# Root rows added by accumulating gathers in the last edge group of a relational graph layer, with a longer count for the group's pace

## The chip, the cores and the metric

One core of one Trainium2 chip. The metric is the device time of one execution in microseconds (us), the median of the runs; before the change it is 1372.6 us over 3 runs (1371.87 to 1372.61).

## The reference, cut to what matters

There are 1250 nodes with 1024 features each, 20000 edges and 8 edge types, all in float32. h is the rectified layer norm of x. For every type r, the rows h[src] of the edges of that type are averaged at each destination node and multiplied by a 1024 x 1024 matrix. The rest is a gate:

```
u   = h @ root + bias + sum over r of mean_r(h[src]) @ weight[r]
z   = concat(u, h) @ w_gate + b_gate
out = x + tanh(u) * z + h * (1 - z)
```

## The kernel before, in words

**Blocks and stages.** The nodes lie in ND = 10 blocks of 128 (the last has 98). TensorE does eleven products of all nodes with one 1024 x 1024 matrix: the eight edge types (stages s = 0 to 7), the root matrix (s = 8), the lower half of the gate matrix (s = 9, its result is called z) and the upper half applied to u (s = 10, the gate stage). Stages 0 to 9 run through `step`, one step for each of NP = 5 pairs of blocks; the gate stage is the loop at the end. Each step is a Strassen-like product in seven parts (`product`, L341): A11, S1, S2, then p3, p7 and p2 (in an order that depends on the step), then A22. After each part `done()` calls the hook `between(j)` with j = 0 to 6, and the hook writes other work into the engines' instruction streams. The instruction order is the program's own; every engine runs its stream in order.

**What the products leave.** Stage results go to DRAM: y for the edge types, `hr_dram` for the root product, `z_dram` for z. Edge types 0 to 4 are one group and 5 to 7 the other; edges of a group are gathered after its products are there.

**Slots.** A node's edges of one group lie in slots, and nodes are sorted by degree, so block d needs K[g][d] slots: for the last group (g = 1) K = 20, 10, 8, 7, 7, 6, 5, 5, 4, 3, in all 75. `add_slot` (L1162) writes one indirect gather on GpSimd (POOL) of 128 rows of y into a tile `got` (L1165), and one multiply-add on VectorE (DVE) that puts it into the block's sum u (L1170). There are GOT = 4 `got` tiles, shared by all gathers of this part, and UB = 4 tiles u.

**The order of the last group.** `edges` (L1188) is a generator; one advance is one tick t, from -1 to 85. It runs through the blocks in the order 4 to 9, then 0 to 3. With starts[b] the first tick of a block, a block's u is read at starts[b] - 5 by `first_u` (a gather from `u_dram`, what the first group left), its slots follow one in each tick, and 4 ticks after the last slot the block leaves through `to`. For blocks 4 to 9 that is `to_last`, a write to `last_dram`. For blocks 0 to 3, which are held on the chip (HELD = 4), it is `add_hr` (L1375): a gather of the block's rows of `hr_dram` into a `got` tile, and three ticks later an addition on DVE (L1380). The starts are ticks 34, 54, 64 and 72 for blocks 0, 1, 2 and 3; block 3's last slot is tick 78, its `hr_dram` gather tick 82, its addition tick 85.

**The pace.** `spread` (L1220) spreads `total` ticks over `parts` calls of the hook: after the k-th of 70 parts (stages 8 and 9, 5 steps of 7 parts each) ceil(total k / 70) ticks have been written, and at the last part all that are left. total is 75 + 2 + 4 = 81; tick -1 is written ahead of it.

**The gate stage.** In the last step of stage 9 `gate_u(0, j)` already reads the rows of h that belong to pair 0 (blocks 0 and 1) into `got` tiles (j = 2), takes tanh of u (L1445) and transposes u on TensorE (L322; j = 3), and subtracts the rows of h from tanh (L1453; j = 4). `gate_bias(0)` (L1418, two writes of b_gate into the place of z) is called there at j = 0. In the gate stage, step i writes: at j = 0 two gathers of `xh_dram` and, by `gate_load(i + 2, 0)`, two loads of u from `last_dram` on SP and two `hr_dram` gathers; at j = 2 the additions L1380 of those, and the rows of h and tanh for pair i + 1; at j = 3 the transposes of pair i + 1. z is added onto the bias by accumulating gathers (L586 with an add, from `z_dram`) at j = 3 of the first step, and j = 0 of the later ones. L373 is the addition that drains part p3 out of its PSUM bank, L381 and L389 those of p7 and p2. Step order in this stage and in the last step of stage 9: A11, S1, S2, p3, p7, p2, A22.

Of the kernel before, what the change touches and what calls it, by code (L numbers as in the profile page):

```python
# [13 lines left out]
OP = mybir.AluOpType  # L14
# [5 lines left out]
def tile_rgcn_highway(  # L20
# [44 lines left out]
    NP = ND // 2  # L65
# [4 lines left out]
    K = ((28, 14, 13, 12, 11, 10, 9, 8, 7, 6), (20, 10, 8, 7, 7, 6, 5, 5, 4, 3))  # L70
# [9 lines left out]
    GOT = 4  # L80
    UB = 4
    LATE = 4
# [7 lines left out]
    def nrows(d):  # L90
        return min(P, N - d * P)
# [4 lines left out]
    def nedges(c):  # L96
        return P if c < NCH - 1 else EL
# [10 lines left out]
    hr_dram = dram.tile([N, D], F32, name="hr_dram")  # L108
# [332 lines left out]
    NM = len(mats)  # L441
# [130 lines left out]
    node = const.tile([P, G, ND], I32, name="node")  # L572
# [11 lines left out]
    def rows_of(to, of, at, op=OP.bypass):  # L584

        nc.gpsimd.indirect_dma_start(  # L586
            out=to, out_offset=None, in_=of,
            in_offset=bass.IndirectOffsetOnAxis(ap=at, axis=0), compute_op=op)
# [53 lines left out]
    with ExitStack() as early:  # L642
# [20 lines left out]
        class Normed:  # L663
# [13 lines left out]
            def spread(self):  # L677
                n = self.n
                nc.vector.bn_aggr(self.mv[:n], self.st[:n].rearrange("p a b -> p (a b)"))
                nc.scalar.activation(self.sd[:n], self.mv[:n, 1:2], AF.Sqrt, bias=eps[:n])  # L680
# [70 lines left out]
        for name, of, pad in (("dst", dst, G * KEYS), ("typ", etype, R), ("src", src, 0)):  # L751
            t = ix0.tile([P, 2, P], I32, name=f"e_{name}")
# [374 lines left out]
        while going[0]:  # L1127
            s, i = next(steps)
# [11 lines left out]
    with ExitStack() as edges_part:  # L1140
# [21 lines left out]
        def add_slot(u, g, d, k, at, w):  # L1162
            n = nrows(d)
            t = got()
            nc.gpsimd.indirect_dma_start(  # L1165
                out=t[:n], out_offset=None, in_=y[g][:, :],
                in_offset=bass.IndirectOffsetOnAxis(ap=at[:n, d, k:k + 1], axis=0),
                bounds_check=y[g].shape[0] - 1, oob_is_err=False)
            w = w[:n, d, k:k + 1]
            nc.vector.scalar_tensor_tensor(u[:n], t[:n], w, u[:n], op0=OP.mult, op1=OP.add)  # L1170

        us = {}

        def new_u(d):

            return upool.tile([P, D], F32, name="u")

        def first_u(g, d):

            n = nrows(d)  # L1180
            u = new_u(d)
            if g == 0:
                nc.sync.dma_start(u[:n], bias[None, :].to_broadcast([n, D]))
            else:
                rows_of(u[:n], u_dram[g - 1][:, :], node[:n, g, d:d + 1])
            return u

        def edges(g, blocks, to, late=0):  # L1188

            nb = len(blocks)
            starts = [late + sum(K[g][d] for d in blocks[:b]) for b in range(nb + 1)]
            leaves = [starts[b + 1] - 1 + GOT for b in range(nb)]
            reads = [max(-1, starts[b] - 5, leaves[b - UB] if b >= UB else -1) for b in range(nb)]
            u, then = {}, {}
            for t in range(-1, leaves[-1] + 4):
                for b, d in enumerate(blocks):
                    if starts[b] <= t < starts[b + 1]:  # L1200
                        k = t - starts[b]
                        add_slot(u[d], g, d, k, idx[:, g], w_of[:, g])
                for b, d in enumerate(blocks):
                    if t == leaves[b]:
                        then[t + 3] = to(d, u[d])
                if then.get(t):
                    then[t]()
                for b, d in enumerate(blocks):
                    if t == reads[b]:
                        u[d] = first_u(g, d)  # L1210
                yield

        def u_back(g):
# [47 lines left out]
        def beside(e, total, s, i, last):  # L1261


            between = spread(e, total, 7 * ((last - s) * NP + NP - i))
            while s <= last:
                step(s, i, between)
                s, i = next(steps, (NM, 0))
            return s, i

        s, i = next(steps)  # L1270
        while s <= EARLY:
            step(s, i)
            s, i = next(steps)
# [17 lines left out]
        while s < R0[1]:  # L1291
            step(s, i, on)
            s, i = next(steps)

        def with_ready(e):

            for _ in e:
                next(ready, None)
                yield

        first_group = with_ready(edges(0, range(ND), u_back(0), LATE))
        next(first_group)
        s, i = beside(first_group, sum(K[0]) + LATE + 1, s, i, R0[2] - 1)
# [4 lines left out]
        with tc.If(passes > 0):  # L1308
# [34 lines left out]
            with tc.For_i(0, passes, 1):  # L1343
# [9 lines left out]
                for c in range(NCH):  # L1353
                    n = nedges(c)
# [13 lines left out]
        LG = G - 1  # L1368
        HELD = 4
# [45 lines left out]
        def gate_bias(i):  # L1415

            for part, d, n in pair(i):
                nc.sync.dma_start(place_of("z", i, part)[:n],  # L1418
                                  b_gate[None, :].to_broadcast([n, D]))
# [19 lines left out]
        def gate_u(i, j):  # L1439

            if j == 2:
                for part, d, n in pair(i):
                    hs[part] = got()
                    rows_of(hs[part][:n], h_dram[:, :], node[:n, LG, d:d + 1])
                    nc.scalar.activation(place_of("d", i, part)[:n], us[d][:n], AF.Tanh)  # L1445
            elif j == 3:
                for part, d, n in pair(i):
                    transposed(h_op[i % 2], part, us.pop(d), n)
                left(h_op[i % 2])
            elif j == 4:  # L1450
                for part, d, n in pair(i):
                    dt = place_of("d", i, part)
                    nc.vector.tensor_sub(dt[:n], dt[:n], hs[part][:n])  # L1453

        def gate_load(i, j):
# [6 lines left out]
            elif j == 2:  # L1462
                while adds:
                    adds.pop(0)()

        blocks = [*range(HELD, ND), *range(HELD)]
        last = edges(LG, blocks, lambda d, u: (add_hr if d < HELD else to_last)(d, u), LATE)
        next(last)
        between = spread(last, sum(K[LG]) + 2 + LATE, 7 * ((NM - 2 - s) * NP + NP - i))
        while s < NM - 1:  # L1470
            def beside_h(j):
                between(j)
                if (s, i, j) == (NM - 2, NP - 1, 0):
                    gate_bias(0)
                if (s, i) == (NM - 2, NP - 1):
                    gate_u(0, j)

            step(s, i, beside_h)
            s, i = next(steps, (NM, 0))

        for i in range(NP):
            t = [rows.tile([P, D], F32, name="row") for _ in range(2)]

            def finish(part, of, c0, more=None):
                d = 2 * i + part
                n = nrows(d)
                at = slice(c0, c0 + of.shape[-1])
                to = t[part][:n, at]
                if more is None:
                    nc.vector.tensor_mul(to, of[:n], place_of("d", i, part)[:n, at])  # L1490
                    nc.vector.tensor_add(to, to, place_of("z", i, part)[:n, at])
                else:
                    nc.vector.tensor_mul(more[:n], of[:n], place_of("d", i, part)[:n, at])
                    nc.vector.tensor_add(to, to, more[:n])
# [38 lines left out]
            if i < NP - 1:  # L1533
                product(h_op[i % 2], fac[NM - 1], t, between=beside_u,
                        last=lambda *of: finish(1, *of))
# [28 lines left out]
```

## Time and profile before

| | |
|---|---|
| median of 3 runs | 1372.6 us |
| the profiled execution's own time | 1373.07 us |
| its span, first to last instruction | 1371.1 us |
| TensorE (PE) matmul busy | 1344.4 us, 98% of the span |
| DVE busy | 944.2 us, 69% |
| POOL busy | 587.3 us, 43% |
| ScalarE (ACT) busy | 370.4 us, 27% |
| mean granted TensorE clock | 0.993 |
| stage 8, 975 to 1096 us | PE busy 121.00 of 121 us, DMA share 0.80 |
| stage 9, 1096 to 1218 us | PE busy 118.94 of 122 us, DMA share 0.66 |
| gate stage and tail, 1218 to 1371 us | PE busy 132.74 of 153 us, clock 0.94, DMA share 0.67 |

In the profile, a line of the timeline gives the start in us, the length in us, the engine, the line of the kernel, the instruction with its tiles, how many were merged, and in square brackets how long the engine had been idle before it and which instruction released it. A waits line gives in total us, how often, and the longest. A windows line gives, for a stretch, its length and then each engine's busy time (with the instruction count in brackets), the granted clock, the busy share of the DMA engines and their rate in GB/s.

### The profile page before, as it was taken

What the parts mean: (1) busy time and instruction counts of PE and PEld (TensorE: products, weight loads), DVE (VectorE), ACT (ScalarE), POOL (GpSimd) and SP (SyncE); (2) the same over time, 40 slices, a digit from 0 to 9 for tenths busy, and PEclk for the clock granted to TensorE, in tenths of its full rate; (3) what the DMA queues carried; (4) which work ended last, traced back from release to release, by engine and by line L of the source; (5) the groups of instructions that cost most, each with busy time, mean ns of one, the idle gap of its engine ahead of it and who ended that gap; (6) DMA issues with size and microseconds to landing.
All of it is one profiled execution on the core that took longest, in us unless ns stands there. A gap on an engine that the chain in (4) does not pass through costs nothing.

```text
span 1371.1 us, 13215 instructions
## 1 busy us (share of the span) xinstructions
PE 1344.4 (98%) x3954; PEld 686.5 (50%) x3954; DVE 944.2 (69%) x1932; ACT 370.4 (27%) x816; POOL 587.3 (43%) x510
## 2 busy tenths in 40 slices
PE   9999999999999999999999999999999999986997
PEld 5444455455445545554554554555455455543443
DVE  6855967876795743426767776877776796656875
ACT  3335566565731111111111111111112111120210
POOL 0001655654562475002444554455356364435641
PEclk9999999999999999999999999999999999998999
DMA  8755766854954351135549689878678936859971
GB/s 306 275 180 149 92 140 142 213 78 116 194 138 109 71 146 22 61 138 184 191 129 329 218 265 354 271 272 294 209 241 317 360 101 219 308 200 280 328 212 58
DMA packets 106908, 271.15 MB, mean 198 GB/s; under 512 B 22692, under 2 KB 24946, under 8 KB 106704
## 3 DMA queue, kind: packets, MB, share of 16 engines
q1 hardware_dynamic: 46640, 120.01, 29.8%
q0 software_dynamic: 44064, 118.28, 27.4%
q10 hardware_dynamic: 16128, 31.98, 7.4%
q8 instruction: 31, 0.51, 0.2%
q14 instruction: 45, 0.37, 0.1%
HBM read 212.71 MB, written 75.66 MB: 210 GB/s over the span
## 4 chain that ended last, share of the span: by engine, by line
PE 75%; issue 9%; DMA 9%; POOL 4%; DVE 2%; SPq 0%; POOLq 0%; ACT 0%; DVEq 0%; ACTq 0%
PE ps L356 60%; PE ps L214 8%; DMA got<-y,idx 6%; PE ps_n L356 3%; DMA got<-hr_dram,node 2%; PE ps_q L214 2%; POOL got L1165 1%; PE ps_n L214 1%; POOL got L586 1%; DMA w<-in_L_gnn_weight_dram 1%; POOL out_dram L592 1%; PE ps_n L903 1%; PE ps L322 0%; POOL h_op L586 0%; POOL w L586 0%
## 5 line engine op out<-in xcount | busy, mean ns | idle before, releaser
L356 PE MATMUL ps<-w,h_op 128*128 128x512 f32 x2512 | 1110.3, 595 | 13.6 <-DVE row L373 11.3
L356 PEld LDWEIGHTS ps<-w,h_op 128*128 128x128 f32 x2512 | 472.7, 191 | 558.2 <-issue 528.4
L1165 POOL DMA_INDIRECT got<-y,idx x193 | 250.6, 1298 | 357.8 <-DVE u L1170 230.8
L1170 DVE SCALAR_TENSOR_TENSOR u<-got,w_of,u 128x1024 f32<-128x1024 f32 (+1 forms) x193 | 247.0, 1282 | 85.5 <-DMA got<-y,idx 82.6
L982 POOL DMA_INDIRECT table<-row_col,at_i x157 | 176.6, 1125 | 157.7 <-DVE at_i L978 73.9
L381 DVE TENSOR_TENSOR row<-row,part 128x512 f32<-128x512 f32 x55 | 37.9, 689 | 123.8 <-ACT part L380 123.8
L429 ACT COPY row<-ps 128x512 f32<-128x512 f32 x50 | 29.3, 585 | 215.5 <-PE ps L356 215.5
L380 ACT COPY part<-ps 128x512 f32<-128x512 f32 x55 | 32.2, 586 | 179.7 <-PE ps L356 179.7
L395 ACT COPY row<-ps 128x512 f32<-128x512 f32 x55 | 32.2, 585 | 175.4 <-PE ps L356 170.7
L214 PE MATMUL ps<-w,w 128*128 128x256 f32 x288 | 71.3, 380 | 0.0
L406 ACT COPY row<-ps 128x512 f32<-128x512 f32 x55 | 32.2, 586 | 139.3 <-PE ps L356 139.3
L214 PEld LDWEIGHTS ps<-w,w 128*128 128x128 f32 x288 | 54.4, 190 | 18.3 <-issue 12.4
L968 DVE SCALAR_TENSOR_TENSOR junk<-k_bc,key_col,before 128x128 f32<-128x128 int32 x157 | 54.9, 350 | 4.2
L908 DVE TENSOR_TENSOR seen<-seen,ps_n 128x100 f32<-128x100 f32 x157 | 40.3, 256 | 24.6 <-PE ps_n L903 20.4
L402 ACT COPY row<-ps 128x512 f32<-128x512 f32 x43 | 25.2, 586 | 115.7 <-PE ps L356 112.1
L214 PE MATMUL ps<-w,h_op 128*128 128x256 f32 x216 | 56.0, 382 | 0.0
L214 PEld LDWEIGHTS ps<-w,h_op 128*128 128x128 f32 x216 | 40.5, 190 | 25.6 <-issue 22.3
L169 DVE TENSOR_TENSOR w<-w,w 128x2048 f32<-128x2048 f32 (+1 forms) x12 | 25.4, 2116 | 39.3 <-PE ps L356 38.2
L885 ACT ACTIVATE is_lo<-io,less_lo 128x128 bf16<-128x128 f32 x157 | 50.2, 391 | 0.7 <-DMA xh_dram<-xt 0.7
L373 DVE TENSOR_TENSOR row<-row,ps 128x512 f32<-128x512 f32 x30 | 20.5, 684 | 37.5 <-PE ps L356 31.3
L623 POOL DMA_INDIRECT node_dram<-ids,pos_i x20 | 28.5, 1426 | 41.1 <-issue 41.1
L356 PE MATMUL ps_n<-w,h_op 128*128 128x512 f32 x96 | 43.2, 592 | 0.0
(215 smaller groups left out, 1183.1 us busy)
## 6 DMA issues: line engine op xcount, KB each, us to landing
y<-row SPq DMA_DIRECT2D x72, 512.0 KB
w<-in_L_gnn_weight_dram ACTq DMA_DIRECT2D x21, 1024.0 KB
w<-in_L_gnn_weight_dram SPq DMA_DIRECT2D x10, 1024.0 KB
k_bc<-keys_dram SPq DMA_DIRECT2D x39, 256.0 KB
l_bc<-los_dram SPq DMA_DIRECT2D x39, 256.0 KB
w<-in_L_gnn_w_gate_dram ACTq DMA_DIRECT2D x6, 1024.0 KB
h_dram<-h_op SPq DMA_DIRECT2D x9, 512.0 KB
u<-in_L_gnn_bias_dram SPq DMA_DIRECT2D x9, 512.0 KB
```

Source lines behind the costliest of these rows:

```text
L214: nc.tensor.matmul(p, a[:, k, :], b[:, k, :], start=(fresh and k == 0), stop=(k == 1), skip_group_check=True)
L356: nc.tensor.matmul(b[:, at], aop[:, i, k, :], w.of[i][:, k, at], start=(fresh and k == 0), stop=(k == KQ - 1), skip_group_check=True)
L380: nc.scalar.copy(d, b)
L381: nc.vector.tensor_add(c22, c22, d)
L395: nc.scalar.copy(c11, b)
L406: nc.scalar.copy(c12, b)
L885: nc.scalar.activation(is_lo[:, i, :], io, AF.Abs, bias=less_lo[:, c0 + i:c0 + i + 1])
L908: nc.vector.tensor_add(seen[j][:, i, :], was, p[:, i, :])
L968: nc.vector.scalar_tensor_tensor(junk, o["k_bc"][:, i, :], key_col[:, c:c + 1], before, op0=OP.is_equal, op1=OP.mult, accum_out=rank[:, c: ...
L982: ins = nc.gpsimd.indirect_dma_start(out=table[:, :], out_offset=bass.IndirectOffsetOnAxis(ap=at_i[:n, i:i + 1], axis=0), in_=row_col[:n, ...
L1165: nc.gpsimd.indirect_dma_start(out=t[:n], out_offset=None, in_=y[g][:, :], in_offset=bass.IndirectOffsetOnAxis(ap=at[:n, d, k:k + 1], axis=0),
L1170: nc.vector.scalar_tensor_tensor(u[:n], t[:n], w, u[:n], op0=OP.mult, op1=OP.add)
```

## The change

`edges` takes a dictionary `more`: a block in it has its u read nine ticks ahead of its first slot instead of five, and four ticks ahead of it `more[d]` is called on u. For blocks 1, 2 and 3 that call is `first_hr`, an accumulating gather of the block's rows of `hr_dram` straight onto u. When these blocks leave, `keep_u` only notes the tile; their `got` tile, the separate gather and the DVE addition are gone. Block 0 keeps `add_hr`. The count of the pace becomes LATE + 75 + GOT + 4 = 87, and `gate_bias(0)` is called at j = 4 instead of j = 0 of the last step of stage 9.

```diff
-        def edges(g, blocks, to, late=0):
+        def edges(g, blocks, to, late=0, more={}):
...
-            reads = [max(-1, starts[b] - 5, leaves[b - UB] if b >= UB else -1) for b in range(nb)]
+            reads = [max(-1, starts[b] - (9 if d in more else 5),
+                         leaves[b - UB] if b >= UB else -1) for b, d in enumerate(blocks)]
...
                     if t == reads[b]:
                         u[d] = first_u(g, d)
+                    if d in more and t == starts[b] - 4:
+                        more[d](d, u[d])
...
+        def with_hr(d):
+            return 0 < d < HELD
+
+        def first_hr(d, u):
+            n = nrows(d)
+            rows_of(u[:n], hr_dram[:, :], node[:n, LG, d:d + 1], OP.add)
+
+        def keep_u(d, u):
+            us[d] = u
+
         blocks = [*range(HELD, ND), *range(HELD)]
-        last = edges(LG, blocks, lambda d, u: (add_hr if d < HELD else to_last)(d, u), LATE)
+        last = edges(LG, blocks, lambda d, u: (keep_u if with_hr(d) else add_hr if d < HELD
+                                               else to_last)(d, u), LATE,
+                     {d: first_hr for d in blocks if with_hr(d)})
         next(last)
-        between = spread(last, sum(K[LG]) + 2 + LATE, 7 * ((NM - 2 - s) * NP + NP - i))
+        between = spread(last, LATE + sum(K[LG]) + GOT + 4, 7 * ((NM - 2 - s) * NP + NP - i))
...
-                if (s, i, j) == (NM - 2, NP - 1, 0):
+                if (s, i, j) == (NM - 2, NP - 1, 4):
                     gate_bias(0)
```

## The prediction

> **What bounds the kernel now.** I began with the busy shares: TensorE is busy for 98% of the span, so whatever is to be won lies in the places where it waits. The waits of PE over the last 372 us are four, and all lie where stage 9 goes over into the gate stage:
>
> ```profile
> PE ps L356 <- DVE row L373: 11.3, 2, 8.8
> PE ps L322 <- DVE u L1380: 2.7, 1, 2.7
> PE ps L356 <- DVE h_op L327: 0.9, 1, 0.9
> ```
>
> Then the timeline of PE there; the brackets hold the idle time and its releaser.
>
> ```profile
> 1204.21 3.60 PE L356 MATMUL ps<-w,h_op 128*128 128x512 f32 x8
> 1210.32 7.13 PE L356 MATMUL ps<-w,h_op 128*128 128x512 f32 x16 [2.50 <-DVE row L373]
> 1218.35 14.00 PE L356 MATMUL ps<-w,h_op 128*128 128x512 f32 x32 [0.90 <-DVE h_op L327]
> 1232.18 1.04 PE L322 MATMUL ps<-ident,u 128*128 128x128 f32 x8
> 1235.94 1.32 PE L322 MATMUL ps<-ident,u 128*128 128x128 f32 x8 [2.72 <-DVE u L1380]
> 1237.06 5.10 PE L356 MATMUL ps<-w,h_op 128*128 128x512 f32 x8
> 1250.97 23.92 PE L356 MATMUL ps<-w,h_op 128*128 128x512 f32 x48 [8.81 <-DVE row L373]
> 1274.72 1.91 PE L322 MATMUL ps<-ident,u 128*128 128x128 f32 x16
> ```
>
> Neither L373 nor L327 is slow; DVE reaches them late, because it runs in order and stands behind something else. The timeline of DVE names it:
>
> ```profile
> 1208.38 1.28 DVE L1170 SCALAR_TENSOR_TENSOR u<-got,w_of,u 128x1024 f32<-128x1024 f32 x1 [4.20 <-DMA got<-y,idx]
> 1216.41 1.28 DVE L1170 SCALAR_TENSOR_TENSOR u<-got,w_of,u 128x1024 f32<-128x1024 f32 x1 [6.14 <-DMA got<-y,idx]
> 1234.66 1.23 DVE L1380 TENSOR_TENSOR u<-u,got 128x1024 f32<-128x1024 f32 x1 [2.71 <-DMA got<-hr_dram,node]
> 1246.60 1.23 DVE L1380 TENSOR_TENSOR u<-u,got 128x1024 f32<-128x1024 f32 x1 [8.51 <-DMA got<-hr_dram,node]
> ```
>
> The first two are the slots of ticks 76 and 77, the third block 3's root rows, the fourth block 4's. On POOL one sees why they come so late: gathers wait for a free `got` tile.
>
> ```profile
> 1217.96 0.99 POOL L1165 DMA_INDIRECT got<-y,idx  x1 [7.03 <-DVE u L1170]
> 1227.50 2.47 POOL L586 DMA_INDIRECT got<-hr_dram,node  x1 [8.54 <-DVE u L1380]
> ```
>
> Of four tiles, block 2's root rows hold one from 1193.90 to 1226.88 and the rows of h two, so the last slots go one at a time. Then everything falls into one stretch. The windows:
>
> ```profile
> 1200.00:1208.00 8.00, 7.81 (x31) 4.06 (x29) 2.62 (x2) 4.39 (x6) 3.10 (x2) 1.00 1.01 391
> 1222.00:1226.00 4.00, 4.00 (x11) 1.78 (x10) 4.00 (x4) 1.02 (x2) 0.00 (x0) 1.00 0.00 0
> 1242.00:1246.00 4.00, 0.16 (x1) 0.00 (x0) 0.00 (x0) 0.59 (x1) 0.00 (x0) 1.00 1.02 401
> 1250.00:1254.00 4.00, 3.03 (x4) 1.49 (x5) 3.83 (x7) 0.00 (x0) 2.80 (x3) 0.50 0.74 233
> ```
>
> At 1222 the DMA engines move nothing; at 1242 they are full. The last line shows a second cost: after the wait of 8.8 us the granted clock is 0.50.
>
> **What these stalls cost.** From one start to the next, against the undisturbed pitch: 56 matmuls from 1302.25 to 1326.29 are 24.04 us, 0.4293 each. p7, p2 and A22 (24 matmuls) take 1218.35 - 1204.21 = 14.14 for 10.30: 3.84 lost. The transposes, 1232.18 to 1237.06, take 4.88, where the next ones take 1302.25 - 1300.50 = 1.75: 3.13. p7 and the wait, to 1250.97, 13.91 for 3.43: 10.48. The next 48 matmuls 23.75 for 20.61: 3.14, the clock alone. Sum 20.59 us.
>
> **The pace.** Before, 81 ticks go over 70 parts, 1.157 each; the last slot (tick 78, the 79th advance) comes at part 68, inside the last step of stage 9, and ticks 81 to 85 in one burst at part 70. With 87, 1.243 each, ceil(87 x 63 / 70) = 79: the last slot is written at part 63, before that step begins, and no burst is left. So L373 and L327 of that step have no slot ahead of them. DVE's lag is to be added: tick 72 was written at part 63 (A22 ends near 1188.7) and done at 1192.7, and slots issued then took 8 to 13 us to land (1189.26 to 1197.85; 1195.29 to 1208.33). I put the last slot at 1193 to 1200; L373 can run from 1202.5 and is needed at 1207.8. The 3.84 go.
>
> In stages 8 and 9 a tick now comes every 2.80 us (122 us / 35 / 1.243) instead of 3.01. By the end of stage 8, 44 advances stand there and not 41: three slots, 3 x 1.28 us of DVE and 1.5 MB. DMA was at 0.96 to 0.99 and 351 to 355 GB/s between 1051 and 1099, so a slot more there (0.5 MB) is 1.5 us of delay. PE hides it: DVE waited for slots up to 4.4 us in stages 8 and 9 before 1204, and PE waited for nothing. Without that cover it costs what it is, 0 to 4.5 us; I take 0, as these rows do.
>
> **The root rows.** Removed: three plain gathers into `got` and three L1380, 3 x 1.22 = 3.7 us of DVE, hidden but for block 3's, the 3.13 above. Added: three accumulating gathers. The nearest rows are those of z:
>
> ```profile
> L586 POOL DMA_INDIRECT h_op<-z_dram,node x6: 1549/1636/2080, 1251.8 to 1324.1; - x6
> ```
>
> 1.64 us of POOL against 1.07 for a plain one: 3 x 0.57 = 1.7 us more, beside 58 of 122 us of POOL in stage 9. Where such gathers run, the full engines move 166 to 248 GB/s, against 391 to 419 with plain ones, so each costs some 1.2 us more of DMA: 3.7 us in a stage whose DMA share is 0.66. An accumulating gather must have the rows of u landed, and POOL's later slots stand behind it. Five slots lie between, 14 us at pace, against landings of 5 to 13 us; with four slots in flight DVE feels nothing. Its own landing has four ticks, 11 us, to block 1, 2 or 3's first slot; z's, issued at 1260.87 and 1262.74, were read at 1269.12 with a wait of 0.3, so 6 to 8 us. Cost: 0, or 3 x 2 = 6 us where a landing of 13 us overruns 11 by 2 and DVE's cover is gone; I take 0, as z's rows are the nearest. `hr_dram` is complete at 1096.7 plus a landing; block 1's rows are asked for at tick 50, part 41, near 1117. The `got` tile that was held is what the last slots lacked.
>
> The Trainium skill speaks against this step: "DMA: Bandwidth & Descriptors", section "Rules for kernel authors", says that an accumulating DMA reads its destination and writes it later, and has to wait for the earlier DMA's semaphore. No run yet shows that wait; taken as one full landing of 13 us for each block and uncovered, it would add 39 us.
>
> **The gate stage's first step.** Blocks 4 and 5 keep L1380, so I follow what they wait for. Their gathers need the two `got` tiles of h, free after L1453. DVE is then at part p7: L381 near 1208.5, L173 2.3 us, L1453 to 1213.7; the gathers leave by 1215. SP's loads of u stand behind the two z writes, and these behind L389 (1214.4) and A22's copy (1215.5); they leave near 1216.5. From 1213 on the queues hold hr, z, u and the next bias, 1 MB each: 4 MB at 390 GB/s end near 1224. L1380 is over by 1227; L373 is first possible at 1228.8 and needed before p2 at 1234. Margin 7 us, against 12.3 us of landing before, when 6.5 MB met. So the 10.48 go, and the 3.14 with them. Late next: step 1's own L1380, now 3 us earlier against p2, since L1453 runs 1.4 us after p2's start instead of 4.5.
>
> The clock term, weighed once more: the skill's "TensorE: Matmul & The Clock Gate", section "Part 1: The HAM clock gate", has the clock halved after an idle window of some 3.4 us. The 0.50 after 8.8 us agrees; 0.74 to 0.83 behind the 2.7 us wait does not. By the rule p7's 1.7 us (5.10 for 3.43) would stay, and the sum be 18.9.
>
> **Gate bias.** On SP nothing stands between j = 0 and j = 4 of that step, and its data are free: it should still leave behind the z writes at 1191. If it did come later, 1 MB less at the peak of 391 GB/s is 2.6 us of landing for others. I take 0.
>
> **Sum.** 1373.07 - 20.6 = 1352.5 us for the profiled execution; it stood 0.5 above the median, so 1352.0.
>
> **Rivals.** (1) Part of the wait before p2 stays, behind block 4's rows. For it: 8.51 us of DVE there, full queues. Against: the margin of 7 us. A rest of 4 us with a clock loss of 3.1 gives 1359; all of it (13.6) 1365.6. Chance 0.20. (2) The quicker pace makes new waits in stages 8 and 9, up to 4.5 us: 1353 to 1357. Chance 0.08. (3) Slower: the accumulating gathers land so late that DVE stands before the first slot of blocks 1, 2 and 3, and PE behind it. PE pays what exceeds 4.4 us; three such waits eat the gain from 4.4 + 20.6 / 3 = 11.3 us each, that is a landing of 22 us; at 25 us three times 14 - 4.4 = 29 us, so 1381. No gather here took over 13 us. Chance 0.06. (4) The pace doesn't bite, because slots go at the rate of four tiles per landing: four in 13 us are 3.25 us a tick, slower than 2.80; the last slots stay where they were, and nothing moves: 1372. Chance 0.04, as most landings are 5 to 9 us. The forecast keeps 0.62.
>
> A measurement of this kernel can tell about 0.2%, 2.7 us, from no change. Faster: 0.62 + 0.20 + 0.08 = 0.90; same 0.04; slower 0.06. The floor is PE without waits, 1352.0, less 1.5 for what the pitch may miss; the range goes up into rival 1, to 1363: 1350.5 to 1363.
>
> **What will show it.** Right: no L1170 on DVE after 1202; seven L1380 instead of ten; PE with no wait over 1 us between 1190 and 1300, the clock 1.00 there; three L586 `u<-hr_dram` near 1117 to 1165, DVE not waiting behind them. Wrong: L373 still releasing PE, a wait for `u<-hr_dram`, or PE waits before 1190.

## The result, and the profile after

The changed kernel takes 1353.43 us (median of 4 executions, 1352.52 to 1362.24), the kernel before beside it 1372.61 us (1371.87 to 1372.80). Three of the four lie at 1352.5 to 1353.9 us and one at 1362.24 us; the record lists two more executions, at 1356.31 and 1363.04 us. The ratio is 0.9886, with a 95% interval of 0.9846 to 0.9926; it is the mean of all six over the mean of the kernel before (1356.83 / 1372.47), while the medians of the four give 0.9860. The profile is of the execution of 1362.24 us (span 1360.2 us), so it shows both what went and what came. These are its waits of PE after 900 us; the columns are total us, times, longest.

```profile
PE ps L356 <- ACT row L402: 4.1, 1, 4.1
PE ps_n L356 <- DVE row L309: 1.6, 1, 1.6
PE ps L356 <- issue: 0.7, 1, 0.7
PE ps_q L214 <- DVE inner L275: 0.5, 1, 0.5
```

No wait for L373, L327 or a root-row addition is left. Three waits are new: L402, L309 and L275; the 0.7 us of issue stand in the kernel before as well. The timeline of PE over the same stretch as before:

```profile
1187.85 13.90 PE L356 MATMUL ps<-w,h_op 128*128 128x512 f32 x32
1205.82 6.54 PE L356 MATMUL ps<-w,h_op 128*128 128x512 f32 x8 [4.08 <-ACT row L402]
1212.19 1.91 PE L322 MATMUL ps<-ident,u 128*128 128x128 f32 x16
1213.94 24.20 PE L356 MATMUL ps<-w,h_op 128*128 128x512 f32 x56
1237.98 1.91 PE L322 MATMUL ps<-ident,u 128*128 128x128 f32 x16
1239.72 24.20 PE L356 MATMUL ps<-w,h_op 128*128 128x512 f32 x56
```

From 1213.94 on, 56 matmuls take 24.04 us, start to start: the whole goes over into the gate stage without a gap, where before 20.6 us were lost. The loss now sits ahead of it: from 1187.85 to 1212.19 40 matmuls take 24.34 us instead of 17.17, so 7.17 us, of which 4.08 are the wait and the rest the clock behind it (eight matmuls in 6.54 instead of 3.60; the granted clock is 0.50 from 1206 to 1209). With 1.57 us for L309 and 0.52 for L275 these are 9.3 of the 9.7 us by which this span exceeds the forecast floor of 1371.1 - 20.6 = 1350.5.

The timeline of DVE shows that the last slot is over at 1201 and that L373 has nothing ahead of it; it is late only because PE is.

```profile
1199.98 1.28 DVE L1170 SCALAR_TENSOR_TENSOR u<-got,w_of,u 128x1024 f32<-128x1024 f32 x1 [0.20 <-DMA got<-y,idx]
1212.45 0.69 DVE L373 TENSOR_TENSOR row<-row,ps 128x512 f32<-128x512 f32 x1 [8.99 <-issue]
1232.15 1.23 DVE L1383 TENSOR_TENSOR u<-u,got 128x1024 f32<-128x1024 f32 x1 [3.74 <-DMA u<-last_dram]
1238.25 0.69 DVE L373 TENSOR_TENSOR row<-row,ps 128x512 f32<-128x512 f32 x1 [1.99 <-PE ps L356]
```

L1383 is L1380 of before. What L402 waited for is told by the chain that ended last (start, us, what):

```profile
1194.94 0.41 DVE row L245
1195.35 0.61 DVE row L309
...
1195.97 9.11 DMA z_dram<-row
...
1205.18 0.59 ACT row L402
...
1205.82 6.54 PE ps L356 x8
```

L402 is ScalarE's copy of part S1 out of PSUM into a row tile. There are four row tiles (`rows`, bufs = 4), two a step. The tile that L402 needs in the last step of stage 9 holds a result of step 2, which is finished only at the end of step 3, by L309, and then written to `z_dram`. Until that write has landed, 9.1 us after SP issued it, L402 can't start; p3 goes on in the bank that L402 reads, so PE stands too. In the kernel before the same write left at 1189.05 and L402 ran at 1195.80, right behind PE:

```profile
1189.05 2.19 SPq L475 DMA_DIRECT2D z_dram<-row  x3
1195.80 0.59 ACT L402 COPY row<-ps 128x512 f32<-128x512 f32 x1 [2.80 <-PE ps L356]
```

L309 is late after the change because DVE has five slots to add just ahead of it, four of them back to back:

```profile
1187.01 5.12 DVE L1170 SCALAR_TENSOR_TENSOR u<-got,w_of,u 128x1024 f32<-128x1024 f32 x4
1193.73 1.28 DVE L1170 SCALAR_TENSOR_TENSOR u<-got,w_of,u 128x1024 f32<-128x1024 f32 x1 [0.68 <-DMA got<-y,idx]
1195.27 0.68 DVE L309 TENSOR_TENSOR row<-row,ps_n 128x512 f32<-128x512 f32 x1
```

DVE comes to these slots late, since ahead of them it had waited longer for others to land. These are its waits for slots between 970 and 1204 us, before and after:

```profile
DVE u L1170 <- DMA got<-y,idx: 36.9, 24, 4.4
DVE u L1170 <- DMA got<-y,idx: 51.2, 23, 7.5
```

### The profile page after: what moved, and what is told of

Same layout as the page of the kernel before. It is cut to its first block, busy times and chain, and to the rows that moved or that the text cites. A ratio compares the mean times of both kernels' runs of the same rounds, so it can differ in the third digit from the quotient of the medians.

```text
span 1360.2 us, 13211 instructions
## 1 busy us (share of the span) xinstructions
PE 1343.3 (99%) x3954; PEld 686.7 (50%) x3954; DVE 940.9 (69%) x1929; ACT 370.2 (27%) x816; POOL 583.6 (43%) x510
## 4 chain that ended last, share of the span: by engine, by line
PE 76%; DMA 10%; issue 8%; POOL 4%; DVE 2%; SPq 0%; ACT 0%; POOLq 0%; DVEq 0%; ACTq 0%
PE ps L356 61%; PE ps L214 8%; DMA got<-y,idx 6%; PE ps_n L356 2%; PE ps_q L214 2%; DMA got<-hr_dram,node 2%; POOL got L1165 1%; PE ps_n L214 1%; DMA w<-in_L_gnn_weight_dram 1%; DVE u L1170 1%; DMA z_dram<-row 1%; POOL got L586 1%; POOL h_op L586 1%; PE ps L322 1%; POOL out_dram L592 1%
## 5 line engine op out<-in xcount | busy, mean ns | idle before, releaser
L1165 POOL DMA_INDIRECT got<-y,idx x193 | 247.3, 1281 | 345.3 <-DVE u L1170 212.1
L1170 DVE SCALAR_TENSOR_TENSOR u<-got,w_of,u 128x1024 f32<-128x1024 f32 (+1 forms) x193 | 246.9, 1282 | 88.8 <-DMA got<-y,idx 86.3
L395 ACT COPY row<-ps 128x512 f32<-128x512 f32 x55 | 32.2, 585 | 163.1 <-PE ps L356 157.9
L406 ACT COPY row<-ps 128x512 f32<-128x512 f32 x55 | 32.2, 586 | 133.3 <-PE ps L356 133.3
L402 ACT COPY row<-ps 128x512 f32<-128x512 f32 x43 | 25.1, 585 | 124.7 <-PE ps L356 108.1
L908 DVE TENSOR_TENSOR seen<-seen,ps_n 128x100 f32<-128x100 f32 x157 | 40.2, 256 | 24.7 <-PE ps_n L903 20.6
L373 DVE TENSOR_TENSOR row<-row,ps 128x512 f32<-128x512 f32 x30 | 20.5, 684 | 47.8 <-PE ps L356 32.2
```

Of the source, the lines that this page charges most:

```text
L395: nc.scalar.copy(c11, b)
L406: nc.scalar.copy(c12, b)
L908: nc.vector.tensor_add(seen[j][:, i, :], was, p[:, i, :])
L1165: nc.gpsimd.indirect_dma_start(out=t[:n], out_offset=None, in_=y[g][:, :], in_offset=bass.IndirectOffsetOnAxis(ap=at[:n, d, k:k + 1], axis=0),
```

## The experiments

Most of the expectations test one theory, their theory A: the quicker pace itself does both, it takes the old waits away, and it makes DVE late with the row results, whose write then holds L402 up. Its rivals put the gain down to the gathers, or the new wait to the moved bias or to other transfers; each expectation says what they would give.

All run on one core, each group beside its own runs of the kernel before on the same chip; the groups' chips differ by up to 3 us in that kernel (medians 1375.4, 1372.3 and 1372.4 us), so ratios are compared across groups, and times only within one.

**The changed kernel again**, unaltered, twice.

> The changed kernel once more, unaltered. Its runs so far lie in two places, 1352.5 to 1353.9 us and near 1362.5, and the one profile is of the upper place: there the ScalarE copy L402 of the last step of stage 9 waited 9.6 us for a write of a row tile to z_dram, PE 4.1 us behind it. Theory A (a late write of the row tile of two steps before, because DVE lags behind slots in step 3 of stage 9, makes the upper place): a lower run has no wait of L402 for that write and no PE wait over 1 us after 1100, and its span is 1350.5 to 1352. Theory B (the upper place is some disturbance of the chip that has nothing to do with this program): the upper runs show longer times everywhere, and the kernel before shows such runs as often.

> The changed kernel unaltered, on the same chip as its variant with the count of 84. Theory A: 1353 to 1363 with a wide spread, its median 0.5 to 5 us over that variant's.

Measured: 1358.25 us (1355.06 to 1360.94), ratio 0.9879 [0.9860, 0.9898], and 1357.95 us (1353.46 to 1362.45), ratio 0.9887 [0.9866, 0.9907]. Over all three groups, with the two further executions, 7 of 16 lie at 1359.9 us or above. It is no pair of fixed places but a scale. The kernel before has one execution of 35 that stands out (1379.89 us, where the rest of its group ends at 1376.9). The first of these profiles has a span of 1353.1 us, PE waits 1.63 us for L402 and for nothing else of note; the second, with 1360.4 us, is like the one above: 4.74 us for L402, 1.83 for L309. As written, theory A's test was missed, since the shorter execution still had the wait of L402 and a span over 1352; what stands is that less of that wait goes with a shorter span, and between these two profiles theory B's general slowness doesn't show.

**Each part alone.** The pace alone is one line on the kernel before; the gathers alone are the change without it and with the bias at j = 0.

```diff
-        between = spread(last, sum(K[LG]) + 2 + LATE, 7 * ((NM - 2 - s) * NP + NP - i))
+        between = spread(last, LATE + sum(K[LG]) + GOT + 4, 7 * ((NM - 2 - s) * NP + NP - i))
```

> The kernel before with the longer count of the pace alone (87 instead of 81); root rows of blocks 1 to 3 still through got tiles and DVE additions, bias at j = 0. Theory A (the pace is what pays: the slots end before the last step of stage 9, and so the got tiles are free there): PE has no wait for L373 or L327 at the end of stage 9, block 3's addition comes at part 69, and the time is 1352 to 1358, with the upper place possible. Theory B (the got tile held by root rows is what cost, and the accumulating gathers pay): the waits for got tiles stay, 1364 to 1370.

> The kernel before with the accumulating gathers for blocks 1 to 3 alone; the count stays 81, bias at j = 0. Theory A (the pace pays): the last four slots still stand in the last step of stage 9 with two of four got tiles held by the rows of h, so PE still waits 2 to 4 us for L373 there, but the tail at part 70 is empty: 1354 to 1362. Theory B (the got tile pays): all four waits go, 1352 to 1354.

Measured: pace alone 1355.99 us, ratio 0.9866 [0.9841, 0.9891]; gathers alone 1365.09 us, ratio 0.9924 [0.9908, 0.9940]. The changed kernel's 0.9879 in the same group doesn't differ from the pace alone. So at this pace the gathers add nothing that can be measured, and without it they bring a little over half (10 of 17 us). The pace alone has a long execution too, 1364.90 us of six, so the accumulating gathers aren't needed for those; no trace of that execution was kept. With the gathers alone PE waits once after 900 us, apart from the 0.7 us of issue, in the gate stage:

```profile
PE ps L356 <- DVE row L373: 5.6, 1, 5.6
```

and POOL shows why: the last slots still stand in the last step of stage 9, two of the four `got` tiles are held by the rows of h, and everything behind them waits for a tile.

```profile
1207.62 1.00 POOL L1165 DMA_INDIRECT got<-y,idx  x1 [6.91 <-DVE u L1170]
1216.57 0.95 POOL L586 DMA_INDIRECT got<-xh_dram,node  x1 [5.49 <-DVE u L1170]
1224.62 2.82 POOL L586 DMA_INDIRECT got<-xh_dram,node  x1 [7.10 <-DVE u L1170]
```

Theory A had the pace right; my place for what stays with the gathers alone was wrong: not 2 to 4 us behind slots at the end of stage 9, but 5.6 behind the root rows of blocks 4 and 5. The time is 3 us above my range, on a chip whose kernel before is 2.7 us longer; by its ratio it would stand at the range's upper end.

**The gate bias**, back at j = 0, or really later: called in the gate stage's first step, behind the loads of u.

```diff
-                if (s, i, j) == (NM - 2, NP - 1, 4):
+                if (s, i, j) == (NM - 2, NP - 1, 0):
                     gate_bias(0)
```

> The changed kernel with the gate bias back at j = 0. Theory A (SP issues it behind the z writes of step 3 in either place, so its place in the program changes nothing): the same two places of times as the changed kernel, difference of the lower ones under 1 us. Theory B (read later, it keeps 1 MB out of the fullest stretch): the bias load starts 10 us earlier than in the changed kernel and the time rises by 1 to 4 us, or the upper place becomes the rule.

> The changed kernel with the first gate bias called in the gate stage (step 0, j = 0, after the loads of u), so that SP cannot issue it before the last z writes, near 1216 instead of 1195 us. Theory A2 (1 MB less beside the row writes of step 3 lets them land sooner): L402 waits some 2 us less than in the changed kernel beside it, the time is 1 to 3 us lower. Theory B2 (the bias stands behind the row writes on its own queue and takes little from them): no difference in L402's wait; the accumulating gathers of z then wait for the later bias, L1436 is late by a few us, and the time is the same or up to 2 us higher.

Measured: back at j = 0 1356.96 us, ratio 0.9866 [0.9843, 0.9889], beside 0.9879 for the changed kernel: no difference. Its executions run from 1354.23 to 1366.91 us; the profile is of the longest, with 3.8 us for L402 and 1.6 for L309, and ahead of 900 us it has 4.5 us of waits (L954, L694 and L222) that the changed kernel's profile doesn't have, in a part that the change doesn't touch. The bias leaves SP right behind the z writes in either place, as in the changed kernel, here SP's timeline:

```profile
1195.97 2.46 SPq L475 DMA_DIRECT2D z_dram<-row  x3
1198.52 1.33 SPq L1421 DMA_DIRECT2D h_op<-in_L_gnn_b_gate_dram  x2
```

Really later (it leaves at 1217.97) gives 1352.65 us, but one execution of five at 1361.16; ratio 0.9870 [0.9850, 0.9891], beside 0.9887 for the changed kernel. The intervals overlap. In its profile the row write takes 7.4 us to land, in those of the changed kernel 7.9 to 9.3; whether the bias has a part in that stays open.

**The pace, both ways.** Count 92 and count 84 in the place of 87, and 84 with the slots started three ticks earlier, so that the last one comes at part 63 as before.

```diff
-        between = spread(last, LATE + sum(K[LG]) + GOT + 4, 7 * ((NM - 2 - s) * NP + NP - i))
+        between = spread(last, LATE + sum(K[LG]) + GOT + 1, 7 * ((NM - 2 - s) * NP + NP - i))
```

> The changed kernel with a count of 92 (1.314 ticks a part), last slot at part 60. Theory A: more lag in stages 8 and 9, PE waits for L309 in step 1 or 2 and for L402 in the last step become the rule: median 1361 to 1370. Theory B: the slots are out of the way still earlier, the same 1355 to 1361 or less.

> The changed kernel with a count of 84 instead of 87 (1.200 ticks a part instead of 1.243); the last three slots then come at parts 64 to 66, in the last step of stage 9. Theory A (DVE's lag behind slots in step 3 of stage 9 makes the write of a row tile to z_dram late, and ScalarE's L402 and PE wait for it; a slower pace lags less): L402 waits under 7 us and PE under 1 us for it, the median is 1 to 3 us below the changed kernel's 1358.3 on this chip, no run above 1360, unless the slots in the last step bring back a wait for L373 of up to 2.5 us. Theory B (the lag does not depend on the pace): the same spread, 1355 to 1361.

> The changed kernel with the last group's slots started three ticks earlier (1 instead of 4) and the count shortened by the same three, 84: the last slot still comes at part 63, at 1.200 ticks a part. Theory A: less lag in step 3 of stage 9 without slots in the last step: PE has no wait over 1 us, median 1352 to 1356, no run above 1360. Against it: the first slots may ask for rows of y that stage 7 has only just written; then DVE stands before them at 985 to 1000 us and PE waits in the first step of stage 8 for up to 5 us.

> The changed kernel with the count of 84 once more, beside the changed kernel itself. Theory A: 1352.5 to 1354 in every run, spread under 1.5 us, since its row writes leave at 1188 and L402 does not wait.

Measured, ratios: count 92 0.9923 [0.9909, 0.9936], 1361.43 us, all five executions above 1360; count 84 0.9859 [0.9844, 0.9874], 1352.81 us (1352.54 to 1353.08); slots earlier 0.9863 [0.9848, 0.9878], 1353.47 us (1352.62 to 1354.76), without the wait of PE near 990 us that I had set against it. Beside the changed kernel on the same chip, count 84 has 1353.15 us, ratio 0.9856 [0.9842, 0.9870], against 1357.95 and 0.9887 [0.9866, 0.9907]; the intervals overlap by 0.0004. Three of its four executions there lie within 1352.6 to 1353.7; the fourth, 1356.94, is the profiled one and has no wait in this stretch, but 2.3 us more in the counting of edges (L903, between 400 and 500 us) and the clock at 0.98 there, in a part that the change doesn't touch; so the spread under 1.5 us was missed. With count 84 L402 follows PE without a wait; ScalarE's and SP's timeline of the first such run:

```profile
1196.03 0.59 ACT L402 COPY row<-ps 128x512 f32<-128x512 f32 x1 [2.80 <-PE ps L356]
```

```profile
1188.25 2.20 SPq L475 DMA_DIRECT2D z_dram<-row  x3
```

Its only PE wait after 900 us is 0.7 us at the end, though its last slots stand in the last step of stage 9; its span is 1350.7 us, the forecast floor to 0.2. With count 92 the same kind of waits lies earlier, at L402 in stage 8 and at L309 in stage 9; PE's timeline:

```profile
1084.51 19.05 PE L356 MATMUL ps<-w,h_op 128*128 128x512 f32 x40 [2.17 <-ACT row L402]
1152.12 5.40 PE L356 MATMUL ps_n<-w,h_op 128*128 128x512 f32 x8 [1.90 <-DVE row L309]
```

In the last step of stage 9, where count 92 has no slots left, its row write leaves early and costs nothing. What grows with the pace is the time that DVE waits for slots. Between 970 and 1204 us, over all profiles, that is 30 to 37 us with count 81, 35 to 39 with 84, 44 to 54 with 87 and 54 with 92; the pace alone, without the accumulating gathers, has 47. So the quicker the slots, the later DVE comes to the row results that stand behind them: theory A.

**One load moved**: the 1 MB load of the gate matrix's quarter b22 behind L402.

```diff
-                if j == 0:
+                if j == (1 if s == NM - 2 else 0):
                     new.load_b22()
-                elif j == 1:
+                if j == 1:
                     new.make_t1()
```

> The changed kernel with one load moved: in the last step of stage 9 the 1 MB load of the gate matrix's lower right quarter is issued at j = 1 instead of j = 0, so on ScalarE it stands behind L402 instead of ahead of it. Theory A2 (the row write takes 7 to 9 us to land because this load, the bias and the slots share the DMA engines with it): L402 waits 2 to 3 us less, PE under 1 us in most runs, median 1353 to 1356, the upper runs become rarer. Theory B2 (the write is late because it is issued late, its landing is not slowed by that load): L402's wait and the time stay, 1355 to 1361; and should the load now come too late for L173, DVE waits there and the time rises.

Measured: 1353.20 us (1352.58 to 1355.55), ratio 0.9860 [0.9845, 0.9875]. No long execution among four, and PE had no wait for L402, though 1.4 us for L309 and 0.8 for L406 in stage 9; but the unaltered kernel didn't run in this group, and the write took 7.5 us to land here too, so it can't be told from a write that left early enough. Open.

**The gathers at the slower pace**: the kernel before with the count 84 alone.

> The kernel before with the count 84 alone, root rows of blocks 1 to 3 through got tiles and DVE. Theory A (the accumulating gathers pay by taking the tail of six ticks away, so that a slower pace is enough): ticks 83 to 85, with block 3's addition, come in a burst at part 70, its root rows are asked for at part 70, and DVE stands before them; PE waits 2 to 3 us for the transposes of block 3 and more behind blocks 4 and 5: 1357 to 1366. Theory B (the gathers pay nothing beside the pace): 1352 to 1354, as with them.

Measured: 1357.36 us (1356.48 to 1358.30), ratio 0.9890 [0.9876, 0.9905], against 0.9856 [0.9842, 0.9870] with the gathers in the same group; the intervals lie apart. Here the gathers are worth 4.2 us: without them PE waits for L373 twice, 2.2 and 1.1 us. The time is in theory A's range; the wait that it put at the transposes of block 3 didn't come.

```profile
1210.19 20.87 PE L356 MATMUL ps<-w,h_op 128*128 128x512 f32 x48 [2.21 <-DVE row L373]
1263.35 20.87 PE L356 MATMUL ps<-w,h_op 128*128 128x512 f32 x48 [1.06 <-DVE row L373]
```

**The profiles side by side.** The row write's issue on SP against ScalarE's L395 of the last step (which follows PE), how long it takes until L402 starts, and PE's wait for L402; a time in us is the span of the profile:

| kernel | write issued, relative to L395, us | issue to L402, us | PE waits, us |
|---|---|---|---|
| count 92 | -5.3 | not waited for | 0 |
| gathers alone (81) | -5.0 | not waited for | 0 |
| count 84 | -4.4 | not waited for | 0 |
| count 84 again, 1355.1 us | -4.4 | not waited for | 0 |
| count 84, slots earlier | -4.0 | not waited for | 0 |
| before | -3.4 | not waited for | 0 |
| pace alone (87) | -3.1 | 7.7 | 0 |
| b22 later | -2.3 | 7.5 | 0 |
| bias behind u | -2.2 | 7.4 | 0 |
| count 84 alone | -1.5 | 7.3 | 0 |
| changed, 1353.1 us | -0.1 | 7.9 | 1.6 |
| count 92, last step of stage 8 | +0.1 | 8.2 | 2.2 |
| changed, 1360.2 us | +1.0 | 9.2 | 4.1 |
| changed, 1360.4 us | +1.6 | 9.3 | 4.7 |
| bias at j = 0, 1365.0 us | +1.7 | 8.3 | 3.8 |

PE asks for p3 6.9 us (two parts) after L395's start, and L402 itself takes 0.6: with a landing of 7.4 us the write must leave 7.4 - 6.3 = 1.1 us ahead of L395. That is where the table turns, between -1.5 and -0.1. Why the late writes also take longer, 7.9 to 9.3 us, no run shows.

## Why the prediction was right, and where it fell short

- **The four old waits** (3.84 + 3.13 + 10.48 + 3.14 = 20.6 us): right as to the waits, and the sum a little high. All are gone, and count 84, which has no new wait, shows what they were worth: 1371.1 - 1350.7 = 20.4 us from profile to profile, but 1372.29 - 1352.81 = 19.5 us from median to median in one group. The 18.9 that was weighed beside it kept p7's 1.7 us; they went too: in the changed kernel that p7 stands in the 56 matmuls from 1239.72 on, which take 24.20 us like the 56 ahead of them. And a pause of 2.2 us was followed by a granted clock of 0.70 with count 92, so a short pause can cost clock here.
- **The median**: in part luck. 1353.43 us lies 1.4 from the forecast because three of the four executions were short; in the two repeats the change gains 17.1 and 14.4 us, not 20.6.
- **The cause**: the forecast called the held `got` tile what the last slots lacked and left the split between the parts open. The runs split it: at the count of 87 the pace alone gives the whole, the gathers alone a little over half; at 84 the gathers add 4.2 us.
- **The gate stage's first step**: right. L1380 was to be over by 1227 with a margin of 7 us; in the run of 1353.1 us it is over at 1229.8, released by u from `last_dram` as followed there, and p2 starts at 1236.0: 6.2 us.
- **The accumulating gathers**: right. 1.56 to 1.83 us of POOL each, forecast 1.64; POOL stood idle 0.30 us of plain issue before each of the three in the changed kernel, and DVE never waited for their rows. The Trainium skill's "DMA: Bandwidth & Descriptors", section "Rules for kernel authors", has an accumulating DMA wait for the earlier one's semaphore; no wait of that kind showed here: the two gathers onto one u are issued 13 to 16 us apart, with five slots between them. The size of their DMA cost wasn't measured alone.
- **The bias**: right, no effect: it leaves behind the z writes, from j = 0 as from j = 4.
- **The pace in stages 8 and 9, taken at 0 and bounded by 4.5 us**: this step failed. By the profiles it costs 0 to 9.7 us from one execution to the next (and 8.3 of span with count 92). The 1.5 us of DMA delay for each slot weren't measured alone; DVE waited for slots 14 us more than before in the long execution. The cover was named wrongly: from PE's silence I had read that DVE may wait 4.4 us at no cost. What ran out was the row tile: DVE's lag delays L309, its result is written later, the write needs 7 to 9 us, and L402 wants the tile. Before, by an estimate from the table, that chain was 2.3 us from costing PE anything (3.4 - 1.1). And the wait is paid more than once, since the clock drops behind it: 4.08 us became 7.17, 4.74 became 7.2.
- **The rivals**: the second is what happened in the long executions, with twice its price; the first, third and fourth were not seen.
- **What was to show it**: no PE wait over 1 us between 1190 and 1300 and the last L1170 by 1202: the second held, the first only in the profiles without the new wait. Of the signs of being wrong, PE waits before 1190 came: 1.57 and 0.52 us.

The best version found is the change with the count 84: 0.9856 to 0.9859 of the kernel before, against 0.9879 to 0.9887 with 87. Its gain over 87 lies mostly in the long executions: none of its eight is above 1357 us.

## What to carry to other kernels

When background work is spread faster so that its tail leaves the critical place, look for what each step's results do afterwards: an output tile that is reused two steps later has a slack of its own, the time from its store's issue to its next writer less the store's landing; here it was some 2 us. Of the paces tried, the best was the slowest one with which the tail is still out of the way; shortening the tail (as the accumulating gathers do) is what lets one choose it. And repeat a kernel whose times lie apart: a scatter of 0.7% was here the scale of one wait.

## What the runs showed of the hardware that was not expected

- A plain 0.5 MB write of a row tile took 7.3 to 9.3 us from issue to the release of its next writer, while the DMA engines moved 313 to 361 GB/s.
- Behind a PE pause the clock is not the same each time: after 2.2 us of waiting 40 matmuls took 19.05 us in one run (1.7 more than at full clock), while 48 behind another pause of 2.2 us took 20.87 (no loss); after 4.1 us eight took 6.54, after 4.7 us 5.91, after 1.9 us 5.40 and after 1.6 us 3.70 (3.60 at full clock).
- Each accumulating gather held POOL 1.56 to 1.83 us in the changed kernel's profile, against 0.95 to 0.98 for the plain gathers of u there; other plain gathers of the stage took 0.95 to 2.50.
